# Adding two channel chunks into one ahead of the mean products of two images' norms, with the products three or four steps later

## The chip, the cores and the metric

The kernel runs on one core of one Trainium2 chip, in float32 throughout. The metric is the device time of one execution in microseconds (us). Before the change it is 2177.85 us, the median of three runs (2172.67, 2177.85 and 2179.22).

The engines are named as in the profile: PE is TensorE (matrix products), DVE is VectorE, ACT is ScalarE, POOL is GpSimd, SP only starts transfers. Each of them works through a queue of its own in order: an instruction that waits holds up all that stands behind it on the same engine, and nothing on another engine unless that engine waits for its result.

## The reference

Four images of 256 channels and 32 x 32 points pass through one layer of a network, and then through a mixture of experts. Cut to what matters here:

```python
def _ln_c(v, eps=1e-6):                      # over the 256 channels
    m = jnp.mean(v, axis=1, keepdims=True)
    s = jnp.var(v, axis=1, keepdims=True)
    return (v - m) / jnp.sqrt(s + eps)

# the layer, for each image (xs: 1024 points x 256 channels)
xn = layernorm(xs, norm_w, norm_b)           # over channels
xm = mamba_v(xc, ...) + skip_scale * xc      # 4 blocks of selective scans
...                                          # gates, 1d convolutions -> xm2
x_local = conv1d(xm2, lc_w, lc_b, groups=Cc, pad=1)
x_global = mha(xm2, ...)                     # 8 heads
x_out = concat([x_local, x_global]) @ fc_w.T + fc_b
x_out = gelu(layernorm(x_out, lgn_w, lgn_b)) # over channels
xi = ln_hw(xi)                               # over the points of a channel
xi = conv2d(xi, dwc_w, groups=Cc) + dwc_b    # 3 x 3, depthwise
x_mixed = layernorm(x_mixed, norm_w, norm_b) # over channels
x_mixed = x_mixed @ proj_w.T + proj_b

# after it
x = x + layer(_ln_c(x))
t = t + ffn(_ln_t(t))                        # the best 2 of 8 experts, 256 -> 1024 -> 256
```

The change is about the means and variances over channels: those of `_ln_c` and the first layernorm (which the kernel does together), of the norm ahead of the gelu, and of the last layernorm.

## The kernel before

**Layout.** Channels lie on the 128 partitions, so an image is two chunks (`NC2` = 2) of 128 channels by 1024 points; work on PSUM goes in halves of 512 points. A sum over channels is a sum over partitions, and the kernel lets TensorE do it: `column_mean` (L430) multiplies a chunk of 128 x 512 with `ones_mean`, a 128 x 128 matrix of 1/256, and adds the product of the second chunk in the same PSUM bank. The mean then stands on all 128 partitions, ready to be subtracted. One mean of one half is therefore two products, one for each chunk. A variance goes the same way, from the squares of the centred chunks. `root` makes 1/sqrt on ScalarE.

**The order.** It is written out by hand. Every stage is a Python generator that issues a few instructions and then yields a number of beats; `beat` advances all the generators that are running, and so fixes in which order instructions enter the engines' queues. `yield 3` therefore means that the work of other stages is issued in between, not that anything waits on the chip. `in_turn` issues a list of products and, two beats behind, what uses them.

**The stages, by image b = 0 to 3.** `normalised(b)` makes the first norm (squares on GpSimd, L543; the scaled copy `xl`, L553; the scaled `xn`, L555 and L558; then taps that are written to HBM). The scans follow: 4 blocks x 2 halves x 16 steps, where each step has an exponential on ScalarE (L715), a product on VectorE (L725), a scan on VectorE (L736) and a product on GpSimd (L744) that TensorE sums (L754). In the middle of each later image's scans, the scans stop for the attention of the image before: `attention(b)` has 32 steps of logits (`st`, L1123), exponentials (`e`, L1133), sums with the values (`av`, L1172); VectorE adds the exponentials of two steps (L1180) for TensorE's sums over the keys (`av<-e,every`, L1144). Beside it `local(b)` makes the taps `xloc` (L470, L475). Then `joined(b)` has the product `fc`, the channel norm and the gelu; `around(b)` the norm over the points and the nine taps of the depthwise convolution on VectorE (L1306 to L1320); `sent_off(b)` the last norm (mean L435, centring L1335, variance, the product with 1/sqrt at L1249), the projection `pr` and the routing of the image to the experts, `experts.dispatch`: transposes (`raw`, L1802), the gate (L1833), the best two of eight by a chain of small instructions on VectorE (L1843 to L1864, L1900 to L1926), the scaled rows `XR` (L1881), the places of each row (`places`, L1869), and 16 indirect DMAs from GpSimd that scatter the rows into a table `XS` in HBM (L1936).

**The variance of the last two norms** is made by `inverse_deviation` (L1209). It squares on ScalarE (L1216) into four tiles of the ring `act2`, and has three ways of putting its instructions into the order: `alone` for image 3, where no other image is left; `quick` for image 1; and one for the rest.

**The experts.** `tiles` runs the expert tiles: rows are fetched (`xs`, L2164 and L2170), transposed on TensorE (`xp`, L2222) and copied by VectorE (`xT`, L2226), multiplied with the first weights (`h`, L2263), passed through a gelu on ScalarE (L2268), multiplied with the second (`y`, L2276), scaled on VectorE (`ys`, L2290 and L2295) and scattered by GpSimd (`Y`, L2303). A tile takes 8 beats, stretched by `PACE` while an image's stages run beside it. Tiles start when the last scan is issued. Series 0 and 1 (8 tiles each) are made of images 0 to 2; tile 8 is the first of series 1 and needs image 2's rows, and the later series need image 3's.

**The end**, where two of the three parts of the change lie: after the scans, `convolutions(3)` and, one after the other, `around(2)` and `sent_off(2)` are issued beside tiles 0 to 4; then tiles are held for `attention(3)` and `local(3)`; then `joined(3)`, `around(3)`, `sent_off(3)` beside tiles 5 to 13; after that there are only tiles:

```python
T["hold",] = True
until("held")
start(flagged(attention(B - 1), "attended", B - 1, 2), local(B - 1))
until("attended", B - 1, 2)
T["hold",] = False
start(one_by_one(joined(B - 1), around(B - 1), sent_off(B - 1)))
drain()
```

`normalised(2)`, the third part, is issued beside `attention(0)`.

## Time and profile before

| what | us | from |
|---|---|---|
| the three runs, median | 2177.85 (2172.67 to 2179.22) | the times |
| the profiled execution | 2175.2 | the times |
| its span in the trace | 2173.3 | the page |
| TensorE, VectorE, ScalarE, GpSimd busy | 1937.3, 1536.4, 1211.4, 1042.7 | the page |
| attention of image 0, with `normalised(2)` | about 440 to 540 | the windows |
| `convolutions(3)` beside `sent_off(2)` and tiles | about 1472 to 1590 | the timeline |
| attention of image 3 | 1590 to 1677 | the timeline |
| `joined(3)` to the end of image 3's routing, beside tiles | 1677 to about 1862 | the timeline |
| tiles alone | about 1862 to 2173 | the timeline |

The page is one execution. TensorE's matmuls are pipelined and their records overlap, so a window with "25.00 of 25" says that TensorE never stood still in it; how much time a group takes is better read from the start of the next one. A row of the timeline gathers neighbouring instructions of one kind; in brackets stand the idle time ahead of it and what ended that. A product of 128 x 512 float32 values leaves two records, so that "x4" is two products.

### The profile page before, as it was taken

The numbers are of one execution on the slowest core, as the hardware profiler recorded it, in microseconds if no ns is written. First come the engines' busy times: TensorE is split into PE (matmuls) and PEld (weight loads), VectorE is DVE, ScalarE is ACT, GpSimd is POOL, SyncE is SP. The second block draws the span as 40 slices with busy tenths as digits, with TensorE's granted clock in tenths as the row PEclk, the third lists the DMA queues.
The fourth block names the chain that finished last, engine by engine and source line by source line (L and its number), as shares of the span: only waits on it lengthen the run. The fifth ranks groups of instructions, "written<-read, shape, count | busy, mean of one in ns | idle before, by whom it ended". The sixth has DMA issues, their size and how long they took to land. (4 is left out here: it accounts for less than half of the span.)

```text
span 2173.3 us, 28179 instructions
## 1 busy us (share of the span) xinstructions
PE 1937.3 (89%) x8690; PEld 867.6 (40%) x8690; DVE 1536.4 (71%) x2231; ACT 1211.4 (56%) x2272; POOL 1042.7 (48%) x930
## 2 busy tenths in 40 slices
PE   6778778999987999988789999679999999999995
PEld 2112112322212332222124223126743668888884
DVE  4989999957998989699898998985364445121111
ACT  4665657668777577776566876524277423222221
POOL 0887887712788850476887026742021113322221
PEclk8888999999999999998999999889999999999997
DMA  3565553401444431154634204344330267866665
GB/s 104 148 156 131 127 123 93 100 28 57 104 117 114 105 73 40 29 138 104 168 81 118 69 22 107 85 164 139 92 82 21 55 189 215 255 182 187 178 159 167
DMA packets 157088, 251.41 MB, mean 116 GB/s; under 512 B 34740, under 2 KB 101332, under 8 KB 156664
## 3 DMA queue, kind: packets, MB, share of 16 engines
q1 hardware_dynamic: 136560, 223.47, 37.6%
q0 software_dynamic: 12720, 17.32, 4.1%
q10 hardware_dynamic: 7640, 8.65, 1.2%
q8 instruction: 72, 1.18, 0.2%
q14 instruction: 96, 0.79, 0.1%
HBM read 137.22 MB, written 36.62 MB: 80 GB/s over the span
## 5 line engine op out<-in xcount | busy, mean ns | idle before, releaser
L744 POOL TENSOR_TENSOR dA<-hs,cs 128x512 f32<-128x512 f32 x512 | 682.0, 1340 | 376.1 <-DVE hs L736 307.6
L715 ACT ACTIVATE dA<-dts,A 128x512 f32<-128x512 f32 x512 | 358.9, 718 | 160.9 <-DMA dts<-dt 66.7
L754 PE MATMUL yp<-dA,quads 128*32 128x512 f32 x1024 | 289.0, 637 | 87.8 <-POOL dA L744 76.0
L2303 POOL DMA_INDIRECT Y<-ys,dest x68 | 109.5, 1610 | 429.6 <-DVE ys L2295 422.5
L1133 ACT ACTIVATE e<-st 128x512 f32<-128x512 f32 x512 | 263.8, 606 | 89.4 <-PE st L1123 88.9
L2268 ACT ACTIVATE hs<-h,b 128x256 f32<-128x256 f32 (+1 forms) x256 | 110.0, 478 | 345.7 <-PE h L2263 233.8
L725 DVE TENSOR_TENSOR dBu<-dts,bs 128x512 f32<-128x512 f32 x384 | 259.6, 677 | 47.4 <-PE bs L707 13.4
L736 DVE TENSOR_TENSOR_SCAN hs<-dA,last,dBu 128x512 f32<-128x512 f32 x192 | 243.6, 1269 | 1.8 <-PE yp L754 1.1
L2276 PE MATMUL y<-w,hs 128*128 128x256 f32 (+1 forms) x1088 | 242.6, 382 | 0.5 <-ACT hs L2268 0.3
L2263 PE MATMUL h<-xT,w 128*128 128x256 f32 (+1 forms) x1024 | 239.6, 390 | 1.1 <-DVE xT L2226 1.1
L736 DVE TENSOR_TENSOR_SCAN hs<-dA,dBu 128x512 f32<-128x512 f32 x192 | 231.6, 1206 | 1.0 <-PE var L435 0.7
L1180 DVE TENSOR_TENSOR e<-e,e 128x512 f32<-128x512 f32 x256 | 168.2, 718 | 77.8 <-ACT e L1133 47.8
L2263 PEld LDWEIGHTS h<-xT,w 128*128 128x128 f32 x1024 | 195.2, 192 | 42.8 <-issue 8.6
L2276 PEld LDWEIGHTS y<-w,hs 128*128 128x128 f32 (+1 forms) x1088 | 197.1, 188 | 37.7 <-issue 10.1
L2226 DVE COPY xT<-xp 128x512 f32<-128x512 f32 (+1 forms) x36 | 23.3, 646 | 250.9 <-PE xp L2222 245.1
L707 PE MATMUL bs<-u,xpwT_s 128*32 128x512 f32 x1024 | 161.2, 660 | 41.3 <-DVE hs L736 18.0
L1123 PE MATMUL st<-qk 32*128 32x512 f32 x1024 | 174.0, 638 | 0.3
L754 PEld LDWEIGHTS yp<-dA,quads 128*32 128x32 f32 x1024 | 50.5, 113 | 303.4 <-POOL dA L744 198.6
L1172 PE MATMUL av<-e,v 128*32 128x512 f32 x1024 | 139.5, 604 | 0.0
L1936 POOL DMA_INDIRECT XS<-XR,to x64 | 65.4, 1021 | 90.3 <-ACT e L1133 53.9
L1123 PEld LDWEIGHTS st<-qk 32*128 32x128 f32 x1024 | 59.5, 183 | 115.3 <-issue 85.6
L1144 PE MATMUL av<-e,every 128*32 128x512 f32 x512 | 85.2, 596 | 2.7 <-DVE e L1180 2.6
(335 smaller groups left out, 2639.1 us busy)
## 6 DMA issues: line engine op xcount, KB each, us to landing
dts<-dt SPq DMA_DIRECT2D x512, 128.0 KB
w<-in_W_dram SPq DMA_DIRECT2D x124, 512.0 KB
cs<-cd SPq DMA_DIRECT2D x512, 64.0 KB
xs<-XS SPq DMA_DIRECT2D x32, 260.0 KB
xd<-xn SPq DMA_DIRECT2D x64, 128.0 KB
xn<-in_x_dram SPq DMA_DIRECT2D x8, 512.0 KB
XL<-xl SPq DMA_DIRECT2D x8, 512.0 KB
xl<-XL SPq DMA_DIRECT2D x4, 1024.0 KB
```

The costliest lines, as they stand in the source:

```text
L707: nc.tensor.matmul(bs[r], xpwT_s[:, n, s : s + 1].to_broadcast([P, 32]), T[b, n, "u"][:, half(h)], start=True, stop=True,)
L715: nc.scalar.activation(dA, T[b, n, h, "dts", g][:, 0, :], AF.Exp, scale=A[:, g, n, q : q + 1])
L725: nc.vector.tensor_tensor(dBu, T[b, n, h, "dts", g][:, 1, :], T[b, n, h, "bs", q], ALU.mult)
L736: nc.vector.tensor_tensor_scan(hs, T[b, n, h, "dA", i], dBu, 0.0 if h == 0 else last, ALU.mult, ALU.add)
L744: nc.gpsimd.tensor_tensor(dA, hs, T[b, n, h, "cs", q], ALU.mult)
L754: nc.tensor.matmul(T[b, n, h, "yp"][ts(g, 32)], quads, T[b, n, h, "dA", q * GD + g], start=False, stop=(q == GS - 1),)
L1123: nc.tensor.matmul(sts[i], k[r, ts(kt, P)], q[r, half(h)], start=True, stop=not shifted)
L1133: ins = nc.scalar.activation(es[i], sts[i], AF.Exp, scale=1.0 / HD**0.5)
L1172: nc.tensor.matmul(accs[0][ts(i, HD)], v8[:, kt, ts(4 * g + i, HD)], es[i], start=(kt == 0), stop=(kt == NK - 1),)
L1180: nc.vector.tensor_tensor(first[i], first[i], es[i], ALU.add)
L2263: nc.tensor.matmul(hp[:, i, :], w1(c, k0 + i), xT[:, c, :], start=(c == 0), stop=(c == NC2 - 1))
L2276: nc.tensor.matmul(yp[ts(k % parts, n), ts(t % 2, C)], hidden(k)[:, ds(t * P, n)], w2(k), start=(k < parts), stop=(k >= NHC - parts),)
```

## The change

Ahead of a mean (or of a variance) the two channel chunks are added element by element, and the sum goes through one product instead of two. Three places:

- `normalised(2)`: GpSimd adds the two chunks into `r1` (allocated earlier for this) and, after the squares, which now go into `r1` and `r2` in place of four `act2` tiles, adds those too. The mean products are issued two beats later, those of the variance one beat later for each half.
- `sent_off(2)`: VectorE adds the two chunks of 1024 points into a new tile `both`, and the mean products follow four beats later; the squares of each half are added on VectorE as well, and their product follows three beats later.
- image 3: `joined(3)` and `sent_off(3)` use the way `alone` of `inverse_deviation`, in which VectorE now adds the squares of both halves one beat after they were issued; and `sent_off(3)` adds its chunks three beats ahead of the mean.

Images 0 and 1, and the norm ahead of the gelu in image 2, stay as they were.

```diff
             r1, r2 = a4(f"r1_{b}"), a4(f"r2_{b}")
+            one_chunk = b == 2
+            if one_chunk:
+                for h in range(2):
+                    nc.gpsimd.tensor_tensor(r1[:, half(h)], part(0, h), part(1, h), ALU.add)
+                yield 2
             yield from in_turn(
-                range(2), lambda h: column_mean(f"mean_{b}_{h}", [part(c, h) for c in range(NC2)]),
+                range(2), lambda h: column_mean(
+                    f"mean_{b}_{h}",
+                    [r1[:, half(h)]] if one_chunk else [part(c, h) for c in range(NC2)],
+                ),
                 centre,
             )
             for h in range(2):
-                sq = [a2(f"sq_{b}_{h}_{c}") for c in range(NC2)]
+                if one_chunk:
+                    sq = [v[:, half(h)] for v in (r1, r2)]
+                else:
+                    sq = [a2(f"sq_{b}_{h}_{c}") for c in range(NC2)]
                 for c in range(NC2):
                     nc.gpsimd.tensor_tensor(sq[c], part(c, h), part(c, h), ALU.mult)
+                if one_chunk:
+                    nc.gpsimd.tensor_tensor(sq[0], sq[0], sq.pop(), ALU.add)
+                    yield 1
                 yield 1
                 var = column_mean(f"var_{b}_{h}", sq)
...
-        def inverse_deviation(name, xc, alone, quick=False):
+        def inverse_deviation(name, xc, alone, quick=False, one_chunk=False):
...
             if alone:
                 sq = [squares(h) for h in range(2)]
                 var = []
+                yield 1
+                for h in range(2):
+                    nc.vector.tensor_tensor(sq[h][0], sq[h][0], sq[h].pop(), ALU.add)
                 for h in range(2):
                     yield 1
                     var.append(column_mean(f"var_{name}_{h}", sq[h]))
...
                     sq = squares(h)
                     yield 1
+                    if one_chunk:
+                        nc.vector.tensor_tensor(sq[0], sq[0], sq.pop(), ALU.add)
+                        yield 3
                     var = column_mean(f"var_{name}_{h}", sq)
...
+            chunks = [xc[:, c, :] for c in range(NC2)]
+            if b >= B - 2:
+                both = a4(f"both_{b}")
+                nc.vector.tensor_tensor(both, *chunks, ALU.add)
+                chunks = [both]
+                yield 4 if b < B - 1 else 3
             yield from in_turn(
-                range(2),
-                lambda h: column_mean(f"mean_{b}_{h}", [xc[:, c, half(h)] for c in range(NC2)]),
+                range(2), lambda h: column_mean(f"mean_{b}_{h}", [v[:, half(h)] for v in chunks]),
                 centre,
             )
-            yield from inverse_deviation(f"fin_{b}", xc, b == B - 1, b == 1)
+            yield from inverse_deviation(f"fin_{b}", xc, b == B - 1, b == 1, b == B - 2)
```

## The prediction

> **What bounds the kernel now.** I read the page first, then the windows of each stage, then TensorE's timeline where it stands still, then VectorE's.
>
> ```profile
> PE 1937.3 (89%) x8690; PEld 867.6 (40%) x8690; DVE 1536.4 (71%) x2231; ACT 1211.4 (56%) x2272; POOL 1042.7 (48%) x930
> ...
> PE   6778778999987999988789999679999999999995
> ...
> DVE  4989999957998989699898998985364445121111
> ```
>
> Each digit is a slice's busy share in tenths. TensorE leads, and in the last third VectorE has room; before that VectorE is as full. The chain of waits ends in the last 1.3 us and says nothing about the middle. So the stages must be read one by one (PE, PEld, DVE, ACT, POOL busy, clock, DMA):
>
> ```profile
> 475.00:500.00 25.00, 25.00 (x165) 7.55 (x164) 12.55 (x18) 21.65 (x43) 4.04 (x3) 1.00 0.06 22
> 625.00:650.00 25.00, 19.25 (x75) 3.71 (x74) 25.00 (x29) 16.45 (x31) 21.33 (x18) 1.00 0.42 106
> 1475.00:1500.00 25.00, 25.00 (x92) 16.75 (x91) 17.37 (x27) 10.70 (x17) 4.98 (x3) 1.00 0.38 109
> 1600.00:1625.00 25.00, 25.00 (x192) 6.89 (x188) 17.30 (x25) 20.67 (x41) 5.94 (x9) 1.00 0.07 23
> 1725.00:1750.00 25.00, 20.23 (x88) 17.06 (x86) 24.38 (x49) 4.84 (x12) 3.35 (x3) 0.93 0.57 160
> ```
>
> Row 1 is attention of image 0 with `normalised(2)` beside it (part A): TensorE is full, GpSimd idle. Row 2 is the scans: VectorE full, TensorE with room. Row 3 is image 2's `sent_off` (B) beside image 3's convolutions and the first tiles, row 4 attention of image 3: TensorE full in both. Row 5 is image 3's tail (C), where TensorE stands still:
>
> ```profile
> 1700.45 1.98 PE L435 MATMUL var_lgn<-sq_lgn,ones_mean 128*128 128x512 f32 x4 [1.60 <-ACT sq_lgn L1216]
> ...
> 1739.69 1.12 PE L2222 MATMUL xp<-ident,xs 128*128 128x128 f32 x4 [3.58 <-DMA xs<-XS]
> 1740.60 4.75 PE L2276 MATMUL y<-w,hs 128*128 128x256 f32 x16
> ...
> 1751.75 2.99 PE L435 MATMUL mean<-xi,ones_mean 128*128 128x512 f32 x4 [2.94 <-DVE xi L1320]
> 1754.53 2.89 PE L2263 MATMUL h<-xT,w 128*128 128x256 f32 x8
> 1757.26 1.88 PE L435 MATMUL mean<-xi,ones_mean 128*128 128x512 f32 x4
> ...
> 1819.40 0.43 PE L1869 MATMUL places<-oh,before 128*128 128x64 f32 x2 [2.15 <-DVE oh L1862]
> ...
> 1845.45 7.17 PE L2263 MATMUL h<-xT,w 128*128 128x256 f32 x32 [0.28 <-DVE xT L2226]
> ```
>
> A row x4 is one pair of products (each leaves two records). Waits named in brackets, with 1.00 before the projection, sum to 11.55 us from 1677 to 1850. After the longer ones the same work is slower: y 4.75 against 3.62 in the tiles before, xp 1.12 against 0.60, mean 2.99 against 1.88, h 2.89 against 1.89, 3.76 us more.
>
> [...] a pair's row lasts 1.88 us, but the next group starts 1.72 later; I price by starts. [...] here gaps of 3.58 and of 2.94 were both followed by slower rows (4.75 for 3.62, 2.99 for 1.88), so a stall costs more than itself. [...] the trace has 676 (L1335) and 1196 to 1218 (L1249). [...] the trace has 1340 ns for 128x512 (L744).
>
> **What goes.** 14 products: A 4, B 4, C 6 (two each for the norm before the gelu, the last mean, the last variance). At 1.72/2 = 0.86 us: 12.0 us of TensorE, 3.4 + 3.4 + 5.2. Six activation table loads of 1.28 go with the new order as well; ScalarE is at 10.70 and 4.84 of 25 there, so I count nothing.
>
> **A.** GpSimd adds four 128x512 tiles, 4 x 1.34 = 5.4 us, in a stage where it works 4.04 of 25: hidden. The squares no longer take four act2 tiles, for which GpSimd waited 19.6 and 12.7 us: a wait without a price, as it had slack. But the chain runs four beats later, and in the new order the second chunk's multiply by r2 (1.2) and one tap (1.2) stand behind the first resumed scan on VectorE, which is full there. GpSimd's scaling of xn follows that multiply, ahead of the next scan products (1.2 to 2.6), into slack of 25 - 21.33. +2.4 taken (0 if the scans have slack, +5 if GpSimd's 2.6 also holds). SP's writes of XL and taps move with it and are needed stages later. A: -3.4 + 2.4 = -1.0 (-3.4 to +1.6).
>
> **B.** VectorE's one 1.2 and two 0.68 adds are covered: 17.37 of 25 busy, then about 9 to 1575. The waits of 4 + 3 + 3 beats are yields: tiles run on and TensorE has work. Their price comes ten beats later. Before, the routing of image 2 ran on an idle VectorE, 1568.7 to 1591.2: gate chain about 4.5 us, eight scalings of XR 2.8, weights 1, places chain 3.3, some 11.6 us. In the new order it stands from the last bias of tile 4 to attention's eighth step, among these:
>
> ```profile
> 1594.22 2.49 DVE L1180 TENSOR_TENSOR e<-e,e 128x512 f32<-128x512 f32 x4 [1.44 <-PE av L1172]
> 1596.63 1.53 DVE L470 TENSOR_SCALAR xloc<-xl,V 128x1024 f32<-128x1024 f32 x2
> 1598.75 2.49 DVE L1180 TENSOR_TENSOR e<-e,e 128x512 f32<-128x512 f32 x4 [0.59 <-PE av L1172]
> ```
>
> Each row of adds feeds TensorE's sums of exponents a pair of steps (5.2 us) later. Counting from attention's start T, on VectorE: ys and gate chain to T+6, two XR scalings, adds of pair 1 to 8.9 (needed 8.0 to 9), XR and xloc, adds of pair 2 at 11.8 to 14.3 (needed 15.3), XR, weights, xloc to 18.5, pair 3 to 21.0 (needed 20.6), places chain and xloc to 26.9, pair 4 to 29.4 (needed about 26.5). So TensorE stands 0.4 and about 2.6, and the places product waits 1.0 for the one-hots behind the fourth value product: 4.0 in all, and TensorE has no slack to win it back. If the chain interleaves better it is 0; fully exposed, 12. Scatters of image 2 (16 on GpSimd, 1.0 each) move from before attention into and past it; tile 8 reads its rows at about 1735, 50 us later. B: -3.4 + 4.0 = +0.6 (-3.4 to +8).
>
> **C.** -5.2 products. VectorE's adds (0.68 x 4, 1.2) stand on the chain of image 3, but tiles fill TensorE meanwhile. By the new order, wait by wait: 1.60 becomes 1.2 (four products of tile 5 now precede the variance); tile 8's table stands two taps (2.3) earlier on VectorE and TensorE is 2.15 early, so 3.58 becomes 1.3, with a new 1.9 for that tile's transposed rows; the mean now follows a half tile more, so 2.94 goes; the projection's 1.00 becomes 0.3; places 2.15 becomes 2.5. Then the new one: image 3's dispatch ends one tile later, and on VectorE two scalings, the places chain (3.3) and the series tables (10.4 us, 1834.2 to 1844.6 before) stand ahead of tile 13's copy to xT: 0.28 becomes 3.1. Waits 10.3 for 11.55, slow rows 2.4 for 3.76 (my estimate: one after xT, one after tile 8). C: -5.2 - 1.25 - 1.35 = -7.8 (-11 to -3). Scatters of image 3 end as late as before (1862.5), tile 16's rows were fetched at 1868.8 for 1885.5; I read some 6 of 13 us margin left: no price.
>
> **Sum.** -1.0 + 0.6 - 7.8 = -8.2. The profiled execution is 2175.2 (span 2173.3 and 1.9 around it): 2167.0. The median of the runs is 2.65 above that execution, so by it 2169.6; I say 2168.
>
> **Rivals.** (1) The full gain: VectorE interleaves without a late sum and no new wait at tile 13. A -3.4, B -3.4, C -11: 2157 to 2159. For it: TensorE full in rows 1, 3, 4. Against: VectorE 25.00 of 25 in the scans. (2) Given back: B and A at half their bad ends (+4 and +0.8), C at its poor end (-3): 2175.2 + 1.8 = 2177. For it: TensorE hands over to in-order queues wherever it gets time. Against: three of the stalls in C have clear reasons to shrink. (3) Slower: one mechanism, routing displaced on VectorE's in-order queue ahead of what TensorE waits for. In attention of image 3 all 12 us are exposed, and four late pairs at 1.1 slow clock each add 4.4: 16.4 instead of 4.0; at tile 13 the tables' whole 10.4 instead of 3.1. 2167.0 + 12.4 + 7.3 = 2187. It decides once the first sum of exponents waits over about 3 us, since the backlog then never drains within the pair's 2.7 us of VectorE slack. Against: the adds stand between pieces of the chain, not behind all of it.
>
> **Chances.** What a measurement can tell from no change is about 0.3%, 6.5 us: faster means below 2171.3, slower above 2184.4. Forecast (2162 to 2174) 0.46, of which 0.05 falls within; full gain 0.15; given back 0.24, within; slower 0.15. So 0.56, 0.29, 0.15. Range 2157 to 2182: it leaves out rival 3 and the tail of rival 1.
>
> **What would show it.** A: 4 fewer products in attention of image 0, resumed scans 2 us longer. B: a wait of `av` (every) for the adds of about 2.6 near the eighth step. C: no wait of the mean for the taps, tile 8's DMA wait near 1.3, a new xT wait of about 3 near tile 13. I am wrong if attention of image 3 lengthens by over 8 us, or if the tiles after 1850 start late for rows not scattered.

## The result, and the profile after

Over 22 runs of each, the changed kernel takes 2182.27 us in the median (2170.5 to 2187.28) and the kernel before 2175.88 (2171.6 to 2180.85). The ratio is 1.0027, with a 95% interval from 1.0017 to 1.0036: slower by 3.7 to 7.8 us, where the prediction's sum of parts had been -8.2. 2182.27 lies just above its range (2157 to 2182).

The profiled execution took 2177.08 us (span 2175.3), only 1.9 more than that of the kernel before. It lies 5.2 below the median of its kernel, so the spans of two single executions don't carry the verdict; I read the stages one by one, and their sizes over several profiles where they vary.

The page of the changed kernel: busy time of the engines, then the two rows of slices.

```profile
PE 1931.4 (89%) x8662; PEld 869.6 (40%) x8662; DVE 1542.6 (71%) x2239; ACT 1204.4 (55%) x2266; POOL 1051.1 (48%) x934
...
PE   6778788999878999987789999679999999999995
...
DVE  3989998867998988799898998984274455121211
```

28 TensorE records are gone, the 14 products foretold, at two records each; 8 instructions are new on VectorE and 4 on GpSimd, and ScalarE has 6 fewer. The work is what the diff says. The windows of the five stages (the same stretches as before, PE, PEld, DVE, ACT, POOL busy, clock, DMA share, GB/s):

```profile
475.00:500.00 25.00, 25.00 (x181) 7.32 (x176) 12.22 (x19) 21.98 (x45) 1.29 (x1) 1.00 0.00 1
625.00:650.00 25.00, 19.69 (x75) 3.90 (x76) 25.00 (x30) 14.29 (x25) 21.27 (x17) 1.00 0.44 107
1475.00:1500.00 25.00, 21.90 (x75) 14.35 (x75) 14.69 (x24) 4.82 (x8) 4.80 (x3) 0.93 0.32 86
1600.00:1625.00 25.00, 24.19 (x168) 6.99 (x165) 20.45 (x45) 17.74 (x35) 2.21 (x4) 1.00 0.04 13
1725.00:1750.00 25.00, 20.48 (x89) 17.18 (x88) 24.38 (x49) 4.85 (x10) 3.29 (x3) 0.93 0.56 168
```

Rows 1, 2 and 5 read as before. Row 3 was full, with 92 records at full clock; now TensorE stands still for 3.1 us of 25, does 75 records, and the clock falls to 0.93. Row 4 had 192 records without a pause, and now has 168 with 0.8 us idle. Both are part B. Lengths of the stages, from the starts and ends of TensorE's rows in the timelines (attention counts from its first logits to the end of its last; the last row runs from there to TensorE's last record):

| stage (us) | before | after | difference |
|---|---|---|---|
| attention of image 0 | 102.1 | 98.0 | -4.1 |
| from there to the first tile (scans), mean of the profiles without and with part A, 12 and 8 | 913.7 | 916.3 | +2.6 |
| convolutions of image 3, `sent_off(2)`, tiles | 140.9 | 142.2 | +1.3 |
| attention of image 3 | 83.1 | 88.9 | +5.8 |
| `joined(3)` to the end | 491.4 | 490.4 | -1.0 |

The sum is +4.6, inside the interval of the timed difference. The scans spread from 910 to 921 us between single profiles, which is why that row is a mean; its 2.6 is still uncertain by some 3. The attentions and the convolutions repeat to 0.4 us where their code is the same. The last row takes 490.4 and 490.9 in two profiles of the changed kernel, and 488 to 492 in the nine that have image 3 as before, so its -1.0 by itself says little more than that the forecast -7.8 is not there.

Where C was to gain, the changed kernel's TensorE timeline of the tail (start, duration, row, the wait ahead of it in brackets):

```profile
1705.09 2.16 PE L435 MATMUL var_lgn<-sq_lgn,ones_mean 128*128 128x512 f32 x4 [1.12 <-DVE sq_lgn L1238]
...
1739.55 0.66 PE L2247 MATMUL xp<-ident,xs 128*128 128x128 f32 x4 [2.07 <-DMA xs<-XS]
1740.04 3.62 PE L2301 MATMUL y<-w,hs 128*128 128x256 f32 x16
...
1746.11 8.70 PE L2288 MATMUL h<-xT,w 128*128 128x256 f32 x32 [2.46 <-DVE xT L2251]
...
1758.54 1.02 PE L435 MATMUL mean<-both,ones_mean 128*128 128x512 f32 x2
...
1807.73 4.14 PE L1858 MATMUL gate<-Wg_c,xr 128*128 128x8 f32 x32
1811.73 3.76 PE L2288 MATMUL h<-xT,w 128*128 128x256 f32 x8
1815.28 4.72 PE L2301 MATMUL y<-w,hs 128*128 128x256 f32 x16
...
1823.94 0.43 PE L1894 MATMUL places<-oh,before 128*128 128x64 f32 x2 [1.77 <-DVE oh L1887]
...
1824.52 3.54 PE L2301 MATMUL y<-w,hs 128*128 128x256 f32 x8
...
1845.57 10.15 PE L2288 MATMUL h<-xT,w 128*128 128x256 f32 x32 [3.26 <-DVE xT L2251]
```

The waits came much as foretold: 1.12, 2.07, 2.46, 1.77 and 3.26 make 10.68, and the mean no longer waits. What was not foretold is the slow rows. Two of them follow a wait (8.70 and 10.15 for 32 records of `h` that take 7.07 elsewhere), and so does the `y` after the places (3.54, where 8 records take 1.89). But `h` at 1811.73 and `y` at 1815.28 follow no wait at all, only the gate's products. The windows around them, columns as above:

```profile
1805.00:1810.00 5.00, 5.00 (x36) 4.66 (x34) 1.10 (x4) 2.47 (x6) 1.92 (x3) 1.00 0.67 132
1810.00:1815.00 5.00, 5.00 (x21) 4.37 (x21) 0.00 (x0) 0.00 (x0) 0.00 (x0) 0.57 0.85 265
1815.00:1820.00 5.00, 5.00 (x20) 4.13 (x19) 1.54 (x7) 2.63 (x5) 0.00 (x0) 0.75 0.58 210
```

TensorE is never idle here, and yet the granted clock falls to half between 1810.7 and 1817.5, by the clock's own record. Between 1680 and 1900 the kernel before is at half clock for 6.8 us, the changed one for 20.5.

Where B lost, TensorE in image 2's `sent_off`, first of the kernel before, then of the changed one:

```profile
1477.53 3.60 PE L435 MATMUL mean<-xi,ones_mean 128*128 128x512 f32 x8
1480.96 1.89 PE L2263 MATMUL h<-xT,w 128*128 128x256 f32 x8
1482.69 1.88 PE L425 MATMUL rp<-d,rpwT_s 128*128 128x512 f32 x4
```

```profile
1476.40 1.10 PE L425 MATMUL rp<-d,rpwT_s 128*128 128x512 f32 x2 [0.77 <-DVE d L459]
1479.83 2.07 PE L425 MATMUL rp<-d,rpwT_s 128*128 128x512 f32 x2 [2.33 <-DVE d L459]
1481.70 2.54 PE L2301 MATMUL y<-w,hs 128*128 128x256 f32 x8
```

and VectorE of the changed kernel at that place:

```profile
1474.98 2.47 DVE L459 SCALAR_TENSOR_TENSOR d<-xm,V,d 128x1024 f32<-128x1024 f32 x2
1477.37 1.22 DVE L1365 TENSOR_TENSOR both<-xi 128x1024 f32<-128x1024 f32 x1
1478.50 1.27 DVE L459 SCALAR_TENSOR_TENSOR d<-xm,V,d 128x1024 f32<-128x1024 f32 x1
```

`rp`, a product of image 3's convolutions, needs VectorE's last tap `d`. Before, the four products of image 2's mean (3.4 us) stood ahead of `rp` on TensorE and gave VectorE time. The change moves them behind `rp`, and puts VectorE's add of 1.2 ahead of that last tap. TensorE now stands 0.77 + 2.33 us, and the two records of `rp` and eight of `y` after that are slow: half clock for 3.4 us from 1479.6.

In attention of image 3, three rows of the changed kernel's TensorE:

```profile
1593.53 0.43 PE L1894 MATMUL places<-oh,before 128*128 128x64 f32 x2 [1.35 <-DVE oh L1887]
...
1601.87 2.33 PE L1137 MATMUL st<-qk 32*128 32x512 f32 x8
...
1613.62 1.09 PE L1137 MATMUL st<-qk 32*128 32x512 f32 x2 [0.81 <-DVE to L1951]
```

The first is the places product foretold. The second is one step's logits (four products), which take 2.33 us where the same step of the kernel before needs 1.35 (`1601.64 1.35`, shown below). The third hints at the cause: logits that wait for `to`, VectorE's last instruction that reads a result of image 2's routing in PSUM. The foretold wait of the sums of exponents isn't there.

### The profile page after: what moved, and what is told of

Read it like the earlier page. It is cut to its first block, busy times and chain, and to the rows that moved or that the text cites. A ratio compares the mean times of both kernels' runs of the same rounds, so it can differ in the third digit from the quotient of the medians.

```text
span 2175.3 us, 28111 instructions
## 1 busy us (share of the span) xinstructions
PE 1931.4 (89%) x8662; PEld 869.6 (40%) x8662; DVE 1542.6 (71%) x2239; ACT 1204.4 (55%) x2266; POOL 1051.1 (48%) x934
## 5 line engine op out<-in xcount | busy, mean ns | idle before, releaser
L2288 PE MATMUL h<-xT,w 128*128 128x256 f32 (+1 forms) x1024 | 244.4, 396 | 6.5 <-DVE xT L2251 6.5
L1137 PEld LDWEIGHTS st<-qk 32*128 32x128 f32 x1024 | 61.4, 183 | 117.1 <-issue 83.1
L739 DVE TENSOR_TENSOR bs<-dts,bs 128x512 f32<-128x512 f32 x128 | 86.1, 673 | 0.7 <-DMA dts<-dt 0.7
```

Source lines behind the costliest of these rows:

```text
L739: nc.vector.tensor_tensor(dBu, T[b, n, h, "dts", g][:, 1, :], T[b, n, h, "bs", q], ALU.mult)
L1137: nc.tensor.matmul(sts[i], k[r, ts(kt, P)], q[r, half(h)], start=True, stop=not shifted)
L2288: nc.tensor.matmul(hp[:, i, :], w1(c, k0 + i), xT[:, c, :], start=(c == 0), stop=(c == NC2 - 1))
```

## The experiments

Each expectation names the theories that it tells apart; theory 1 is the one that I held at that time. Ratios are against the kernel before, run on the same chip. Diffs are against the changed kernel, where nothing else is said.

**The three parts alone.** e1 has only `normalised(2)`, e2 only `sent_off(2)`, e3 only image 3; each leaves the other two as they were before.

```diff
# e1
-            if b >= B - 2:
+            if b < 0:
# e2
-            one_chunk = b == 2
+            one_chunk = b < 0
-            if b >= B - 2:
+            if b == B - 2:
# e3
-            one_chunk = b == 2
+            one_chunk = b < 0
-            if b >= B - 2:
+            if b == B - 1:
```

(With them the adds of the variances: e1 and e2 have none in `alone`, e1 and e3 none for image 2.)

> Only the part in normalised(2): GpSimd adds the chunks and the squares; sent_off and joined as before. Theory 1 (stalls and half-clock windows of image 2's and 3's tails make the change slow): this part is a small gain, 1.5 to 4 us faster than before (ratio 0.998 to 0.9995): 3.4 us of products go from attention of image 0, 1 to 2.4 come back in the resumed scans. Rival (the loss is in the scans, where VectorE is full): no gain or slower, 0 to +4 us.

> Only the part in sent_off(2). Theory 1: slower than before by 4 to 9 us (ratio 1.002 to 1.004). TensorE waits about 3 us for VectorE's taps of image 3's convolutions (rp<-d) where the four mean products stood before and covered that wait, then runs at half clock for 3.4 us; attention of image 3 is 5 to 6 us longer, because image 2's routing is now on VectorE beside it. Rival (TensorE keeps the 3.4 us of products): 1 to 3 us faster, attention of image 3 as long as before.

> Only joined(3) and sent_off(3). Theory 1: about as before, -3 to +2 us: 5.2 us of products go, and half-clock windows between 1680 and 1870 us grow from 6.8 to 14 or more us (one at the 16 gate products that stand in one block, one after the late xT of tile 13). Rival (the waits alone count, and they sum to about as much as before): 5 to 8 us faster.

Measured: e1 0.9999 (0.9985 to 1.0013), e2 1.0028 (1.0016 to 1.004), e3 0.9967 (0.9951 to 0.9983). In us -0.3, +6.1 and -7.2. A is worth nothing that can be measured (1.5 to 4 faster had been expected), B carries the loss as expected, and C alone brings about what the prediction had forecast for it: for e3 the rival had the number, not theory 1. Their sum, -1.4, is 7.3 us short of the whole's +5.9. The four figures together are uncertain by some 5.6, so C seems to lose in company. The single profiles point the same way: `joined(3)` to the end takes 486.7 us in e3, 4.6 less than before, and 490.4 in the whole.

**The gate's block.** In the whole, the 32 records of image 3's gate stand together on TensorE; before and in the next experiment they stand in two groups with a tile's products between them.

```diff
# e4, e18
-                yield 1
+                yield (2 if t == 3 else 0) if b == self.B - 1 else 1
```

> The changed kernel with image 3's gate products in two groups again, a part of a tile's h between them, and what follows on the same beats. Theory 1 (a block of 128x8 products counts as idleness to the clock): no half-clock window at the gate, about 3 us faster than the changed kernel, ratio against before about 1.001. Rival (the window there has another reason, or falls elsewhere instead): half clock near the gate as in the changed kernel, and no gain, ratio about 1.003.

> The changed kernel once more, on the same chip as its version with the gates apart. If half-clock windows at the gate belong to it: one of 3.4 or 6.8 us at about the gate products again, more than 13 us at half clock between attention and 1900 us, ratio against before 1.002 to 1.0035. If they were chance in the one profile: none there, 7 to 10 us at half clock.

> The changed kernel with image 3's gate products in two groups, once more, beside the changed kernel on the same chip. If the block of gate products matters in the whole change: 3 to 6 us faster than it (ratio against before 0.9985 to 1.001), no window at the gate. If not: within 1.5 us of it.

e17 is the changed kernel once more, e18 is e4 once more, on the same chip as each other. Measured: e4 0.9999 (0.9985 to 1.0012), e18 1.0009 (0.9996 to 1.0022), e17 1.0026 (1.0014 to 1.0038). e18's median is 5.2 us below e17's, and the tail takes 482.4 and 482.9 us in e4 and e18, 490.9 in e17. The timeline and a window of e17, then the timeline of e18:

```profile
1808.87 4.04 PE L1858 MATMUL gate<-Wg_c,xr 128*128 128x8 f32 x32
```

```profile
1812.00:1817.00 5.00, 5.00 (x15) 4.19 (x15) 0.00 (x0) 0.44 (x2) 0.00 (x0) 0.50 0.78 233
```

```profile
1820.17 1.85 PE L1858 MATMUL gate<-Wg_c,xr 128*128 128x8 f32 x16
1821.87 1.97 PE L2288 MATMUL h<-xT,w 128*128 128x256 f32 x8
1823.68 1.85 PE L1858 MATMUL gate<-Wg_c,xr 128*128 128x8 f32 x16
1825.38 3.70 PE L2301 MATMUL y<-w,hs 128*128 128x256 f32 x16
```

e17 repeats the changed kernel's result. With the block in one piece the half-clock time follows it again, for 6.8 us; in two pieces, the same products are followed by rows at full speed, twice. From 1680 to 1900 half clock takes 6.8 us in e4 and in e18 against 20.5 in both profiles of the changed kernel, so the difference is more than the gate's own 6.8: less half clock comes later in the tail, too.

Whether the block is enough by itself was tried in the kernel before:

```diff
# e9, against the kernel before
-                yield 1
+                yield (0 if t == 3 else 2) if b == self.B - 1 else 1
```

> The kernel before with one thing changed: image 3's two groups of gate products are issued in one block, the part of a tile that stood between them comes after. Theory 1 (a block of 32 records of 128x8 products, about 4 us, counts as idleness to TensorE's clock): a new half-clock window of 3.4 or 6.8 us within 5 us of the block, 1 to 4 us slower than before (ratio 1.0005 to 1.002). Rival (the windows at the gate in the changed kernel came from something else that it moved): no new window there, ratio 1.000.

e9 took 1.0004 (0.9991 to 1.0017). Its timeline and, below it, the window after its block:

```profile
1804.50 3.64 PE L1833 MATMUL gate<-Wg_c,xr 128*128 128x8 f32 x32
1807.99 3.70 PE L2276 MATMUL y<-w,hs 128*128 128x256 f32 x16
```

```profile
1805.00:1810.00 5.00, 5.00 (x38) 4.79 (x38) 0.93 (x5) 0.82 (x1) 0.00 (x0) 1.00 1.01 328
```

The block stands there, and the clock stays at 1.00. In e3, with the block in one piece too (3.63 us), 3.4 us of half clock follow. So half clock followed the block in three of the four profiles that have it (twice for 6.8 us, once for 3.4), and followed the gate in none of the seven that have C with the gate in two groups (e4, e18 and, below, e7, e8, e10, e11, e15).

The kept traces narrow the reason. In each of the 20 profiles every half-clock stretch starts a whole multiple of 3.413 us after the one before it (the changed kernel's at 1479.6, 1745.8, 1810.7, 1824.3 and 1844.8, that is 78, 19, 4 and 6 multiples), and these marks lie differently against the kernel's first instruction from profile to profile (the first one after it comes at 1.61 us in the changed kernel's, at 2.10 in that of the kernel before). I cut TensorE's time at these marks and took of each piece the share that holds no product, with the narrow products of the gate and of the places counted as none:

| profile | gate's products | pieces with them: start, share | half clock next |
|---|---|---|---|
| changed kernel | one block | 1807.3: 81%; 1810.7: 31% | 6.8 us |
| e17 | one block | 1808.5: 85%; 1811.9: 24% | 6.8 us |
| e3 | one block | 1802.3: 9%; 1805.7: 88% | 3.4 us |
| e9 | one block | 1802.6: 38%; 1806.0: 59% | none |
| e4 | two groups | 1814.5: 45%; 1818.0: 45% | none |
| e18 | two groups | 1818.6: 45%; 1822.0: 45% | none |

Over all 20 profiles, from 1440 to 1900 us, each of the 73 full-clock pieces with a share of 60% or more is followed by half clock, 8 of the 24 between 50 and 60%, and none of some 2500 below. So in these traces it is the share of one such piece that counts, not the length of one wait, and e9's block escaped because it fell across two pieces. That narrow products count like idle time is inferred from this fit; no run moved a block against the marks alone. The same wait can therefore cost or not. Here are the places and what follows them in e4 and in e8 (described below), where the 1.77 us fall into two pieces (38% and 28%) and into one (66%):

```profile
1828.65 0.43 PE L1894 MATMUL places<-oh,before 128*128 128x64 f32 x2 [1.77 <-DVE oh L1887]
...
1829.15 1.95 PE L2301 MATMUL y<-w,hs 128*128 128x256 f32 x8
```

```profile
1815.37 0.43 PE L1894 MATMUL places<-oh,before 128*128 128x64 f32 x2 [1.77 <-DVE oh L1887]
...
1815.86 2.67 PE L2301 MATMUL y<-w,hs 128*128 128x256 f32 x8
```

One profile is thus one draw of the marks' position, 20.5 against 6.8 us included; what the block costs on average is told by the times alone.

**C by itself, mended.** e7 is e3 with the gate in two groups. e8 also issues the series tables (10.4 us on VectorE) after the next tile's copies to `xT`, instead of ahead of them:

```diff
# e8
-                if experts.placed and wide not in tables:
+                if experts.placed and wide not in tables and len(got.get(n, ())) > 4:
```

> joined(3) and sent_off(3) alone, with image 3's gate products in two groups with a part of a tile's h between them. Theory 1 (the block of 128x8 products halves the clock): no half-clock window at the gate, 1.5 to 4 us faster than that part with one block, ratio against before 0.995 to 0.996. Rival (its window is chance): ratio 0.9967 as before.

> As the kernel with the gates apart, and the tables of the last two series are made after tile 13's transposed rows are copied, not before. Theory 1 (xT of tile 13 waits behind 10 us of tables on VectorE): the wait of h for xT at about 1840 falls from 3.2 to under 0.5, the half-clock window after it goes, 4 to 6 us faster than without, ratio 0.992 to 0.994. Rival (something else is late there, xp or the rows): the wait stays at 2 to 3, or goes to the next tile.

e7 took 0.9974 (0.9962 to 0.9986), no better than e3, where 1.5 to 4 us had been expected. In its trace the half clock at the gate is gone, but 3.4 us of it follow the wait of the places instead (from 1816.8), so that both profiles have 10.2 from 1680 to 1900. e8 took 0.9957 (0.9939 to 0.9974), where 0.992 to 0.994 had been expected. In its trace the wait of `h` for `xT` of tile 13 (2.37 us in e7) is gone and the tail is 4.3 us shorter than e7's, so the tables' place on VectorE's queue is the cause of that wait, as the prediction had it. (By the times e8 is 3.7 us faster than e7, not clear of noise.)

**B: the last tap.** e6 is e2 with the add of the chunks on GpSimd, out of the queue of the tap:

```diff
# e6
-                nc.vector.tensor_tensor(both, *chunks, ALU.add)
+                nc.gpsimd.tensor_tensor(both, *chunks, ALU.add)
```

> The part in sent_off(2) alone, with the two chunks added on GpSimd in place of VectorE, same beats. Theory 1 (VectorE's 1.2 us add stands ahead of the last tap that TensorE waits for, on top of the cover that went): rp's wait falls from 3.1 to 1.9 or less, the half-clock window after it may go, 1 to 3 us faster than with VectorE, ratio against before 1.0015 to 1.0025; attention stays at about 89. Rival (only the missing cover of the four mean products counts): wait still 3.1, ratio 1.003.

e6 took 1.001 (1.0001 to 1.0018) against e2's 1.0028: about 3.9 us of 6.1 are won back, uncertain by some 3. The view of its waits from 1450 to 1700, a group, its sum, count and the longest:

```profile
PE rp L425 <- DVE d L459: 2.1, 2, 1.3
```

In e2 the same group reads 3.1, 2 and 2.3. One microsecond of wait went, with it the half clock after it, and the stage takes 139.6 us instead of 142.1. In e2 the waits fill 68% of one piece between the marks, in e6 at most 47%. The 2.1 that stay I put down to the absent cover of the mean products; no run put that cover back alone. Attention of image 3 stays at 88.9.

**B: attention of image 3.** e5 takes out the three beats after the add of the squares, so that image 2's routing comes sooner, six beats in all for the two halves:

```diff
# e5, e2's parts and
                         nc.vector.tensor_tensor(sq[0], sq[0], sq.pop(), ALU.add)
-                        yield 3
                     var = column_mean(f"var_{name}_{h}", sq)
```

> The part in sent_off(2) alone, with the variance's products right after VectorE's adds: 4 beats later in all in place of 10, so that the gate, the one-hots and the places product of image 2 stand ahead of attention again. Theory 1 (the displaced routing makes attention of image 3 longer): attention back from 88.9 us to 83 to 85, 4 to 6 us faster than with 10 beats, ratio against before 1.000 to 1.001; the wait of rp for VectorE's taps stays at about 3. Rival (attention is longer for another reason): still about 89 us, ratio 1.003.

Attention is back to 84.3 us: it is the routing's arrival within it that costs. But the stage ahead takes 151.4 instead of 142.1, with new waits of the places (2.5) and of the last variance (2.3) and 10.2 us of half clock besides the 3.4 at its start; in all 1.0034 (1.002 to 1.0048). Against the 1.000 to 1.001 expected, the beats can't simply be taken out again: what attention gets back, the stage ahead loses, and more.

What of the routing costs attention? e12 takes the eight scalings of image 2's rows off VectorE, e13 takes the routing's scratch out of PSUM (two of its banks, for the gate's and the places' results, held until VectorE has read them), and e16 does both. e12, e13 and e16 are e2 and these:

```diff
# e12 and e16
-                nc.vector.tensor_scalar(
+                (nc.gpsimd if b == self.B - 2 else nc.vector).tensor_scalar(
# e13 and e16
+            if b == B - 2:
+                experts.scratch = a4(f"scratch_{b}")
...
+        scratch = gp if b != self.B - 2 else self.scratch[:, 0:HALF]
...
+        if b == self.B - 2:
+            held, cp = cp, self.scratch[:, HALF : 2 * HALF]
+            nc.vector.tensor_copy(cp[:, 0 : 2 * W], held[:, 0 : 2 * W])
```

e14 is the kernel before, where two small products more take two banks at the start of attention of image 3, and VectorE frees them in steps 7 and 9:

```diff
# e14, against the kernel before
+            kept = []
+            if b == B - 1:
+                for k in range(2):
+                    kept.append(ps(f"kept_{k}"))
+                    nc.tensor.matmul(
+                        kept[k][:, 0:8], ones_mean, ones_mean[:, 0:8], start=True, stop=True
+                    )
...
+                if kept and at in (6, 8):
+                    one = small.tile([P, 8], F32, tag="kept", name=f"one_{at}", bufs=1)
+                    nc.vector.tensor_copy(one, kept.pop()[:, 0:8])
```

> The part in sent_off(2) alone, with image 2's eight scalings of XR (2.8 us on VectorE) on GpSimd, which is idle there. Theory 1 (attention of image 3 is longer because VectorE's queue is full from its start for 28 us): attention falls from 88.9 to 85.5 to 87.5 us, ratio against before 1.0015 to 1.0025. Rival (not VectorE's amount of work but the order of the places product and of ScalarE's ex sets it): attention stays within 0.5 of 88.9, ratio 1.003.

> The part in sent_off(2) alone, but image 2's routing keeps its scratch in SBUF: the gate's PSUM bank is free after the first VectorE instruction that reads it, the bank of the places products after one copy. Nothing else moves; VectorE has one copy of 0.3 us more. Theory 2 (attention of image 3 is longer because the displaced routing holds two of the eight PSUM banks that its logits turn through): attention falls from 88.9 to 84 to 86.5 us (the wait of the places product, about 2, stays), ratio against before 1.0005 to 1.002. Theory 1 (VectorE's amount of work): attention stays at 88.9 or grows.

> The kernel before, with no routing moved: at the start of attention of image 3 two products of 128x8 columns are made into two PSUM banks that nothing needs, and read by two small VectorE instructions in the seventh and the ninth step, which frees them. Theory 2 (two banks held): attention grows from 83.1 to 85 to 88 us, 2 to 4.5 us slower (ratio 1.0008 to 1.002). Theory 1: attention grows by at most 0.3 us, ratio 1.000.

> The part in sent_off(2) alone, with image 2's routing scratch in SBUF and its scalings of XR on GpSimd: both limits in attention of image 3 taken away at once. Theory 3 (two limits lie one behind the other, the two PSUM banks and VectorE's queue, and either alone keeps most of the 5.8 us): attention falls to 84.8 to 85.6 us, only the wait of the places product (2.0) is left. Rival (a third reason): attention stays above 86.5.

e12 took 1.003 (1.0018 to 1.0042), no better than e2, with attention at 88.8. GpSimd's and VectorE's timelines of e12, one row each:

```profile
1595.87 16.75 POOL L1903 TENSOR_SCALAR XR<-XR,mv,r 128x256 f32<-128x256 f32 x8
```

```profile
1602.78 2.70 DVE L1194 TENSOR_TENSOR e<-e,e 128x512 f32<-128x512 f32 x4 [1.34 <-PE av L1186]
```

VectorE now stands idle for 1.34 us and waits for TensorE, not the other way round, and attention is as long as before the edit. With that my first theory, VectorE's amount of work, fell. VectorE's last read of the routing's results in PSUM, `to`, ends 25.6 us after attention's start in e12 as in the changed kernel. (The move also makes the rows later, 2.1 us for each on GpSimd, so e12 alone doesn't clear VectorE of every part.)

What holds TensorE there is held banks. Rows of `st` in the timeline of the kernel before:

```profile
1601.64 1.35 PE L1123 MATMUL st<-qk 32*128 32x512 f32 x8
```

and of e14:

```profile
1609.65 2.31 PE L1123 MATMUL st<-qk 32*128 32x512 f32 x8
...
1615.82 1.84 PE L1123 MATMUL st<-qk 32*128 32x512 f32 x8
```

e14 displaces no routing, and shows the slow logits of the changed kernel (2.31 there, 2.33 here), with attention at 85.3 instead of 83.1; 1.0006 (0.9994 to 1.0017) by the times, which can't tell 2 us. The kernel's ring of banks in PSUM has eight (`bufs=8`), tiles of 128 x 512 float32 values, and an `st` product of 128 x 512 fills one. One step's logits take four and the two running sums `av` two, so that normally two are left to begin the next step, and with two more held none; this much is read from the code. e13 is the other side: from its third row of logits to its ninth it runs near the pace of the kernel before (8.12 to 24.06 us after its start, 15.9, where the kernel before takes 15.5 and the changed one 19.5). Free banks win back 3.5 of these 4.0 us; the rest of the 5.8 is for the most part the places product, its wait of 1.35 and its own time. But e13 too has an attention of 87.9 and 1.0028 (1.0018 to 1.0038), since now this wait shows in its timeline:

```profile
1622.42 1.07 PE L1186 MATMUL av<-e,v 128*32 128x512 f32 x8
1624.01 2.85 PE L1158 MATMUL av<-e,every 128*32 128x512 f32 x8 [0.52 <-DVE e L1194]
```

A group of sums that takes 1.04 us elsewhere starts 0.52 late and lasts 2.85: some 2.3 us, near the prediction's "about 2.6". In the changed kernel this wait isn't there; my reading is that the banks hold TensorE back so far that VectorE's lateness never shows, so that one cost stands before the other.

e16 was to take away both and to bring attention near the kernel before's; it took 88.6 and 1.0023 (1.0014 to 1.0033), above the 86.5 that its expectation had set for a third reason. From the fifth row of logits to the ninth it runs at the old pace (10.4 us), but the places product waits 1.98 us (1.15 in e13), half clock for 3.4 us follows, and the sums of pair 4 are still 1.3 late. The longer wait comes from VectorE's chain ahead of it, of which some small instructions take up to 0.51 us where e13's take 0.17 to 0.23; GpSimd's rows start beside them. In e12, with the same rows on GpSimd and the scratch in PSUM, those ahead of the places take 0.16 to 0.23, and why they are slower here wasn't tried. So of B's 5.8 us in attention the held banks are shown as one cause. That the late sum is the next is argued, as no version of B came out without both.

**All together.** e10 is the changed kernel without B (`sent_off(2)` as before), with e4's gate and e8's tables. e11 is the whole change with e4's gate, e8's tables and, for image 2, e6's add on GpSimd. e15 is e11 with e13's scratch.

```diff
# e10
-            if b >= B - 2:
+            if b == B - 1:
-            yield from inverse_deviation(f"fin_{b}", xc, b == B - 1, b == 1, b == B - 2)
+            yield from inverse_deviation(f"fin_{b}", xc, b == B - 1, b == 1)
# e11 and e15
-                nc.vector.tensor_tensor(both, *chunks, ALU.add)
+                (nc.vector if b == B - 1 else nc.gpsimd).tensor_tensor(both, *chunks, ALU.add)
# e10, e11 and e15
-                if experts.placed and wide not in tables:
+                if experts.placed and wide not in tables and len(got.get(n, ())) > 4:
-                yield 1
+                yield (2 if t == 3 else 0) if b == self.B - 1 else 1
```

> normalised(2), joined(3) and sent_off(3) as in the changed kernel, sent_off(2) as before, image 3's gate products in two groups and the last tables after tile 13's copy. Theory 1: the parts add up, 9 to 14 us faster than before (ratio 0.9935 to 0.996), attention of image 3 at 83.1 us, and no wait of h for xT at tile 13. Rival (normalised(2) spoils the tail, as the sum of single parts against the whole could say): ratio 0.997 or above.

> The whole change, with image 2's chunks added on GpSimd, image 3's gate products in two groups and the last tables after tile 13's copy. Theory 1: the waits and windows named so far are the whole loss but for attention's 5.8 us, so 3 to 7 us faster than before (ratio 0.9967 to 0.9986), attention of image 3 still at 89. Rival (more is lost than has been named): ratio 0.999 or above.

> The whole change with all that was mended (image 2's chunks on GpSimd, image 3's gate products in two groups, the last tables after tile 13's copy), and image 2's routing scratch in SBUF. Theory 2: 2.5 to 4.5 us faster than without the last (ratio against before 0.995 to 0.9958), about as fast as leaving sent_off(2) alone (0.9938). Theory 1: ratio 0.9968 as without.

e10 took 2164.05 us (2158.21 to 2169.2), 0.9938 (0.9918 to 0.9958): faster than both kernels. TensorE's wait for `xT` in it, from 1680 to 1900:

```profile
PE h L2288 <- DVE xT L2251: 2.7, 1, 2.7
```

where the changed kernel has two such waits, 2.46 and 3.26: that of tile 13 is gone. e11, with B in its mended form, took 2170.01, 0.9968 (0.9954 to 0.9982), 6.0 us more than e10 on the same chip, with attention at 88.9 against e10's 83.1: the two differ in B alone, and by the stages that is +5.8 in attention, -1.2 ahead of it and -0.8 behind. e15 was to be 2.5 to 4.5 us better than e11 and isn't, 0.9987 (0.9974 to 1.0, on another chip): attention is 1.0 shorter, but the tail 8.4 longer, with waits of `y` (0.80 and 3.17) that no instruction of the trace ends, and with 13.7 us at half clock between 1680 and 1900 against e11's 3.4. The scratch takes a tile of a ring that others use; whether that is the cause wasn't tried.

## Why the prediction was wrong

In short, B was put at +0.6 and is worth about +6, C was put at -7.8 and is worth about nothing in the whole; together they are most of the distance from -8.2 to what was measured.

**A is not contradicted.** -3.4 and +2.4 had been put down. Attention of image 0 is 4.1 shorter and the scans 2.6 longer in the mean, -1.5 by the stages, and e1 measures -0.3 with some 3 us either way; the forecast of -1.0 lies within, but so does nothing at all.

**B failed first at the sentence "VectorE's one 1.2 and two 0.68 adds are covered".** It looked at how busy VectorE was, 17.37 of 25, and not at who waits for what stands behind the add. It is the tap `d`, and behind it `rp`. The step also took the removed products as time won, while the four of them were the cover of that tap: 3.4 us removed from in front of `rp` came back as 3.1 of wait, with a stretch of half clock. Against the -3.4 credited, the stage is 1.3 longer. e6 returns part of it by the queue alone.

**B failed again in the term "4.0 in all"**, by size and by cause. Attention lengthened by 5.8. The wait of the places for the one-hots was 1.35 where 1.0 was foretold. The sums' 0.4 and 2.6 don't show; the logits are held back instead, some 4 us between the third and the ninth row, by the two PSUM banks in which the gate's and the places' results wait for VectorE. The prediction moved VectorE's instructions and not the buffers that they free. e14 makes the same rows slow with banks alone, and e13, with the banks free, brings out a late sum of about the foretold size. So B is +7.1 by the stages and +6.1 by e2, for +0.6.

**C was right in its waits, and failed in the term "slow rows 2.4 for 3.76"**, which came to 9.3. The products went (-5.2), the waits are 10.68 for the 10.3 foretold, that of the mean is gone, the places' is 1.77 for 2.5, tile 8's DMA wait is 2.07 for 1.3, its transposed rows 2.46 for 1.9, tile 13's 3.26 for 3.1. The slow rows, each against the same work at full clock:

| row | after | full clock | more |
|---|---|---|---|
| `h` x32 after the wait for tile 8's `xT` | 8.70 | 7.07 | 1.63 |
| `h` x8 after the gate | 3.76 | 1.89 | 1.87 |
| `y` x16 after it | 4.72 | 3.62 | 1.10 |
| `y` x8 after the places | 3.54 | 1.89 | 1.65 |
| `h` x32 after tile 13's `xT` | 10.15 | 7.07 | 3.08 |

9.3 in all: 6.9 more than foretold, which is the distance between -7.8 and the tail's -1.0. The term had counted one slow row for each of two places, going by the slow rows after the idle gaps of 3.58 and 2.94 in its lines. What counts in the traces is 60% of a 3.41 us piece without full products, which brings in the rows after the places and after the gate. How large the term comes out is in part luck: the same code has slow rows or none by where the marks fall (as the wait of 1.77 in e4 and in e8).

By the times, which average over that, the whole less A and B leaves about 0 for C, uncertain by some 4, against -7.2 for C alone (e3). Two groups in place of the block win back 6.1 us (e4 against the changed kernel) and 5.2 (e18 against e17, on one chip), with a tail 9.0 shorter than before in e4; each is uncertain by some 4. But e3 has the block too and keeps its gain, and e7 wins nothing over e3. So the block's cost in the whole is shown, its size is not settled, and why C kept its gain alone stays open.

**The rivals.** Rival 3 had the sign: VectorE's in-order queue did delay what TensorE waits for (the add out of its queue took 1.0 of 3.1 us of wait at the tap away in e6, the tables behind the copies the 2.37 at tile 13 in e8), but the places of it were the last tap and PSUM's banks, not the exposed chain of 12 us and the tables' 10.4. Its 2187 is 4.7 too high. "I am wrong if attention of image 3 lengthens by over 8 us" was not met by 5.8, and the tiles after 1850 were not late for rows (no wait of TensorE shows from 1850 to 2000): the prediction's own tests didn't look at the two places at which it failed.

What stays open: why C kept its gain alone and not in the whole; what the third cost of B in attention is that e16 met; and why e15 lost.

## What to carry to other kernels

Before you take away products that "cost TensorE time", see which late operand they hid (here 3.4 us of products went and 3.1 of wait came): ask what stands next in TensorE's queue, and whether it would have been ready. Where a chain of small instructions moves into a stage with full PSUM traffic, count the banks that it holds until it ends (freeing two won 3.5 us back in e13's rows), not only the time that its instructions take on their engine. And look at the granted clock around each changed place, in more than one profile: rows that are slow without any wait are part of the bill (8.48 us here for 5.51, after the gate), and where they fall can change from one execution to the next.

## What had not been expected of the hardware

- In the changed kernel the clock fell to half for 6.8 us with TensorE never idle in the windows' account, after 32 records of products only 8 columns wide that took 4.1 us. In two groups of 16, 1.85 us each, nothing of the kind followed directly in seven profiles (e4, e7, e8, e10, e11, e15, e18).
- Half-clock stretches start on marks 3.413 us apart that run on through the whole execution and lie differently in each. Of 3.41 us between two marks, 60% without full products (idle, or only the gate's and the places') was followed by half clock in all 73 cases of the 20 profiles from 1440 to 1900 us, less than 50% in none of some 2500.
- Half clock followed gaps that are shorter than the 3.58 and 2.94 of the prediction's lines: 0.77 and 2.33 before `rp` in the changed kernel, 1.98 in e16 before the places. The 1.77 before the places was followed by it in e8 and not in e4.
- Subtracting one pointer scalar (a value for each partition) and multiplying by another, on 128 x 256 float32 values, takes GpSimd 2.1 us (16.75 for eight in e12) and VectorE 0.40 (the median before, L1881): five times, where a product or sum of two tensors of 128 x 512 takes GpSimd 1.34 (L744) and VectorE 0.68 (L1180), twice.
